# Where the slot numbers of a token sorting are computed: four instructions go from VectorE to GpSimd, and the sorting's parts are dealt out over the steps in another way

## The chip, the core and the metric

The kernel runs on one core of a Trainium2 chip. A core has TensorE (matrix products and transposes), VectorE, ScalarE and GpSimd (elementwise work and reductions), and SyncE, whose queue issues most DMAs. In the profile they are PE, DVE, ACT, POOL and SP; PEld is TensorE's loading of weights. The metric is device time of one execution in microseconds.

## The reference

A block of two layers on x of 2 x 2048 tokens of 512 features, with a context of 2 x 128 tokens. Each layer adds an attention over the context and a feed-forward part. Layer 0's feed-forward is quantised; layer 1's sends each token to one of eight experts:

```python
x = x + _L0_xattn_ref(_layernorm(x), ctx, ctx, ...)      # rope, tanh, causal, 16 heads of 64
x = x + _L0_ffn_ref(_layernorm(x), ...)                  # fake-quantised silu(gate) * up
x = x + _L1_xattn_ref(_layernorm(x), ctx, ctx, mask, ...)  # 16 heads of 32
x = x + _L1_ffn_ref(_layernorm(x), Wg, bg, We, be)

def _L1_ffn_ref(x, Wg, bg, We, be):
    probs = jax.nn.softmax(x @ Wg + bg, axis=-1)         # 512 classes
    idx = jnp.argmax(probs, axis=-1)
    p = jnp.take_along_axis(probs, idx[..., None], axis=-1)[..., 0]
    e_idx = idx % 8                                      # the expert of a token
    h = jax.nn.relu(jnp.einsum('bsd,edf->besf', x, We) + be[None, :, None, :])
    onehot = jax.nn.one_hot(e_idx, 8)
    return jnp.einsum('besf,bse->bsf', h, onehot) * p[..., None]
```

## The kernel before

The 4096 tokens are 32 tiles of 128 (`NT = 32`). Layer 0 comes first, then layer 1's attention, one tile per step of the loop `for n in range(NT)` (L1226), then the experts. The profile's steps below are this loop's n.

**A step of layer 1's loop.** `scores(n)` makes 16 heads' scores on TensorE (L892), and VectorE takes them from PSUM with the mask (L900) and finds the maxima (L905), each in two halves. `exponentials(n)` is on ScalarE (L914). `shares(n, half)` sums on VectorE (L920, first half only), takes reciprocals (L922), and multiplies on GpSimd (L923, one instruction per half). `turned(n)` transposes the result on TensorE (L116) and copies it back on ScalarE (L931), `mixed(n)` applies it to the values (L941). In between stand the work of tiles before and after: `queries` for the next block of two tiles (L872), `projected(n - 1)` (L955, L956), `biased(n - 1)`, which adds a bias on GpSimd (L949), `normed2(n - 1)` and `normed(n + 4 or n + 5)` (L92, L94, L100 and L821 on VectorE, with a power on GpSimd in L101 between them), `split` and `joined` (L826 on VectorE, a transposing DMA L829, L832 on ScalarE), `logits`, `picked` and `gated` for tile n - 2 (L978, L984 to L1008). `gated` ends in a reciprocal (L1008) and the write of the tile's row to `x_dram`; its count of tokens per expert is one GpSimd instruction (L1004). L1008 is the last of VectorE's ordinary instructions in a step.

**The sorting.** Tokens have to be gathered by expert. It is done twice: `routing(True)` (L1050) for the first 22 tiles (`NTA`), over the last steps of the loop, and `routing(False)` for all 32, during the experts. `routing` is a Python generator, and each `yield` ends one part. In `routing(True)` the parts are:

1. Ranks by three matmuls (L1056 to L1059), copied to SBUF (L1061, L1063).
2. Tiles per expert and their sums, on 8 columns (L1030 to L1073; L1030 and L1031 are a helper that divides and rounds down).
3. Which expert each gathered tile has (L1085 to L1092).
4. The slot numbers on 128 x 22 x 8 (L1096 to L1099), their sum over the experts (L1100), and its quotient and remainder (L1030, L1031, L1102) on 22 columns.
5. Two parts with one-hot rows of the quotient (L1111, L1115, L1118 each).
6. Three parts with one-hot rows of the remainder (L1124: twice 1024 columns, then 768).
7. 22 matmuls that turn these into token numbers (L1132) and four small instructions (L1134 to L1138).

The caller, at the end of a step, deals the parts out: three at step 24, two at each step after. So step 24 has parts 1 to 3; step 25 has 4 and the first of 5; step 26 the second of 5 and the first of 6; step 27 the other two of 6; step 28 has 7, and then the first four gathers (`gathered`, L1149, issued by GpSimd).

**What sets the order.** TensorE, VectorE, ScalarE and GpSimd work in manual order (`manual_schedule`): each engine's instructions stand in the order in which the Python code emits them, and each engine takes them strictly in turn. A part of the sorting that step n emits at its end is therefore ahead of everything of step n + 1 on its engine. The buffers of the sorting are columns of token tiles that have already been written to `x_dram` (`part`, L1017), so no other work shares them.

Of the kernel before, what the change touches and what calls it, by code (L numbers as in the profile page):

```python
# [19 lines left out]
ALU = mybir.AluOpType  # L20
# [4 lines left out]
P = 128  # L25
# [11 lines left out]
NE = 8  # L37
# [5 lines left out]
NTA = 22  # L43
# [6 lines left out]
NOWHERE = float(2**20)  # L50
# [13 lines left out]
def two_layers(ctx: ExitStack, tc: tile.TileContext, a, out):  # L64
    nc = tc.nc
# [85 lines left out]
    with ExitStack() as l0:  # L151
# [176 lines left out]
        def normed(k):  # L328


            stats[k] = small.tile([P, NB0, 2], F32, name="stat")
            for t, n in enumerate(tiles[k]):
                mv = variance(xs[n])
                ve = small.tile([P, 1], F32, name="ve")
                nc.vector.tensor_scalar(ve, mv[:, 1:2], 1.0 + EPS, EPS * EPS, ALU.mult, ALU.add)
                nc.vector.tensor_copy(stats[k][:, t, 0:1], mv[:, 0:1])
                nc.gpsimd.tensor_tensor(stats[k][:, t, 1:2], ve, minus_half, ALU.pow)
            if k > 1:
                features_in(k)
                turned_in(k)  # L340
# [42 lines left out]
        def queries(u, par):  # L383

            k, g = divmod(u, NG)
            j, b = blocks[k]
            if par == 0:
                if j not in tabs:
                    tables_in(j)
                ropes[u] = [mid.tile([P, B0], F32, name=f"rt{i}", bufs=1) for i in range(4)]  # L390
            pq, rt = psm.tile([P, B0], F32, name="pq", tag="m"), ropes[u]
            for c in range(ND):
                nc.tensor.matmul(  # L393
                    pq, wqs[c // 2][:, c % 2, par, g * P : (g + 1) * P], xnTs[k][:, c, :], start=(c == 0), stop=(c == ND - 1)
                )
            cos, sin = tabs[j]
            if par == 0:
                nc.vector.tensor_tensor(rt[0], pq, cos, ALU.mult)  # L398
                nc.vector.tensor_tensor(rt[1], pq, sin, ALU.mult)
                return  # L400
            qs[u] = [mid.tile([P, B0], F32, name=f"q{i}") for i in range(2)]
            nc.vector.tensor_tensor(rt[2], pq, sin, ALU.mult)  # L402
            nc.gpsimd.tensor_tensor(qs[u][0], rt[0], rt[2], ALU.subtract)  # L403
            nc.vector.tensor_tensor(rt[3], pq, cos, ALU.mult)
            nc.gpsimd.tensor_tensor(qs[u][1], rt[3], rt[1], ALU.add)

        def scores(u):

            k, g = divmod(u, NG)
            j, b = blocks[k]  # L410
            for par, k_ in ((0, kTe), (1, kTo)):
                for h in range(4):
                    rows = slice(32 * h, 32 * h + 32)
                    nc.tensor.matmul(  # L414
                        sc[:, h, :B0], k_[rows, g, b * T : (b + 1) * T], qs[u][par][rows, :],
                        start=(par == 0), stop=(par == 1), tile_position=(32 * h, 0),
                    )
            prs[u] = pr = mid.tile([P, 4, B0], F32, name="pr")
            nc.scalar.activation(pr, sc[:, :, :B0], AF.Tanh, scale=1.0 / (math.sqrt(DH0) * GROK))  # L419

            nc.scalar.activation(pr, pr, AF.Exp, bias=pad[:, b : b + 1], scale=GROK)
            if j == 0:
                nc.gpsimd.affine_select(
                    out=pr[:, :, :P], in_=pr[:, :, :P], pattern=[[0, 4], [1, P]],
                    compare_op=ALU.is_ge, fill=0.0, base=0, channel_multiplier=-1,
                )
# [60 lines left out]
        with tc.manual_schedule(engines={E.PE, E.DVE, E.Activation, E.Pool}):  # L487
# [20 lines left out]
            for u in range(nu + 2):  # L508
# [34 lines left out]
                if g in (0, NG - 1) and u > 1:  # L543
                    if makes and not loaded:
                        load_, args, _, _ = makes[0]
                        loaded.append(load_(*args))
                    elif makes:
                        _, _, make, args = makes.pop(0)
                        turns[u + 1] = make(loaded.pop(), *args)
                        if makes:  # L550
                            load_, args, _, _ = makes[0]
# [63 lines left out]
    hot = w1.tile([P, NT, NE], BF16, name="hot")  # L615
# [21 lines left out]
    with ExitStack() as up:  # L637
# [100 lines left out]
        for blk in range(NT // NBF):  # L738
            for i in range(NI):
# [20 lines left out]
                n = (blk + 1) * NBF + t  # L760
# [3 lines left out]
                if i >= 3 and i % 2 == 1:  # L764
                    n = (blk + 1) * NBF + (i - 3) // 2
# [182 lines left out]
    def biased(n):  # L948
        nc.gpsimd.tensor_tensor(xs[n], xs[n], bob, ALU.add)  # L949
# [67 lines left out]
    def part(n, shape, dtype=F32, at=0):  # L1017

        size = math.prod(shape)
        v = xw[n][:, at : at + (size * mybir.dt.size(dtype) + 3) // 4]  # L1020
        if dtype is not F32:
            v = v.bitcast(dtype)[:, :size]
        if len(shape) == 1:
            return v
        names = "abc"[: len(shape)]
        return v.rearrange(f"p ({' '.join(names)}) -> p {' '.join(names)}", **dict(zip(names, shape)))
# [6 lines left out]
    def along(k):  # L1033

        return part(16, [NE], at=NE * k)
# [14 lines left out]
    def routing(first):  # L1050

        nt, nj = (NTA, NJA) if first else (NT, NJB)
# [7 lines left out]
        rank = part(15, [nt, NE])  # L1060
        nc.vector.tensor_copy(rank, prank)  # L1061
        cnt, tl, base = along(1), along(2), along(3)
        nc.vector.tensor_copy(cnt, pc)  # L1063
        yield
        if first:
# [8 lines left out]
            base = start  # L1074
# [18 lines left out]
        yield  # L1093
        slot, pos, sj, ss = part(20, [nt, NE]), part(16, [nt], at=128), part(16, [nt], at=192), part(16, [nt], at=256)
        limb = lim.unsqueeze(1).to_broadcast([P, nt, NE])
        nc.vector.tensor_tensor(slot, rank, limb, ALU.is_ge if first else ALU.is_lt)  # L1096
        nc.vector.scalar_tensor_tensor(slot, slot, NOWHERE, rank, ALU.mult, ALU.add)
        nc.vector.tensor_tensor(slot, slot, base.unsqueeze(1).to_broadcast([P, nt, NE]), ALU.add)
        nc.vector.tensor_tensor(slot, slot, hot[:, :nt, :], ALU.mult)  # L1099
        nc.vector.tensor_reduce(pos, slot, AX.X, ALU.add)  # L1100
        floor_div(sj, pos, P)
        nc.vector.scalar_tensor_tensor(ss, sj, -float(P), pos, ALU.mult, ALU.add)  # L1102
# [123 lines left out]
    for n in range(NT):  # L1226
        blk, t = n // NB1, n % NB1
        ahead = blk + 1 < nblk
        fs = range(t * ND // NB1, (t + 1) * ND // NB1)
        if n > 0:  # L1230
            biased(n - 1)
        firsts = [m for m in (n + 2 * NB1, n + 2 * NB1 + 1) if m < NT and (m >= TURNED) == (m > n + 2 * NB1)]
        firsts = [normed(m) for m in firsts]
        scores(n)
        if 4 <= n < 4 + 2 * NE and n % 2 == 0:

            nc.scalar.dma_start(out=rowadd, in_=v_dram[(n - 4) // 2].partition_broadcast(P))

        late = t == 0 and n > 1
        if ahead and not late:  # L1240
            queries(blk + 1, fs[:1])
        if late:
            logits(n - 2)
        exponentials(n)
        if ahead and late:
            queries(blk + 1, fs[:1])
        if n == 0:
            for i in range(NT - held, NT - held + 2):
                down(i)
                widened(i + 2)  # L1250
        shares(n, 0)
        if n > 1:
            if not late:
                logits(n - 2)
            picked(n - 2)
        shares(n, 1)
        if n > 0:
            projected(n - 1)
            normed2(n - 1)()
        firsts = [first() for first in firsts]  # L1260
        rest = gated(n - 2) if n > 1 else None
        if n + 1 < NT:
            kept_keys(n + 1)
        for first in firsts:
            if first:
                first()
        if 0 < n <= NE:
            load(we[:, n - 1], a["L1_ffn_We"][n - 1].rearrange("(c p) f -> p c f", p=P))
        if ahead:
            queries(blk + 1, fs[1:])  # L1270
        if n == 0:
            for i in range(NT - held + 2, NT):
                down(i)
            dwn.close()
            ffd.close()
            moe = ctx.enter_context(tc.tile_pool(name="moe", bufs=1, side="right"))
            we = moe.tile([P, NE, ND, D], F32, name="we")
        if 4 <= n < 4 + 2 * NE:
            e, half = divmod(n - 4, 2)
            for c in range(2 * half, 2 * half + 2):  # L1280
                nc.gpsimd.tensor_tensor(we[:, e, c, :], we[:, e, c, :], rowadd, ALU.add)
        if not ahead:

            expert(n - NT + NB1)
        turned(n)
        if rest:
            rest()
        if n > 0:
            turned2(n - 1)
        mixed(n)  # L1290
        if t == NB1 - 1 and blk + 2 < nblk:
            for t in range(NB1):
                turned1((blk + 2) * NB1 + t)
        if n == NTA + 2:
            route = routing(True)
        if route:
            for _ in range(3 if n == NTA + 2 else 2):
                if next(route, route) is route:
                    route = None
                    for j in range(4):  # L1300
                        gathered(j)
                    break
        if n == NT - NB1 - 1:
            for j in range(3):
                centered_x(j)
            turned_x2(0)
# [59 lines left out]
```

## Time and profile before

| | |
|---|---|
| median of 3 runs | 1602.42 us (1600.16 to 1602.53) |
| the profiled execution | 1603.67 us, its span 1601.9 us |
| busy in the span | TensorE 97%, VectorE 74%, ScalarE 45%, GpSimd 36% |
| layer 0 and its feed-forward, up to the first score matmul of layer 1's loop | 0 to 930.44 us |
| steps 0 to 23 of that loop | 930.44 to 1302.31 us |
| steps 24 to 27 | 1302.31 to 1371.06 us |
| steps 28 to 31 | 1371.06 to 1434.75 us |
| last logits and experts | 1434.75 to 1601.9 us |

All times inside the trace are counted from the start of the span. TensorE's busy share says little on its own, since a matmul that waits in the pipeline counts too. What one step of the loop costs is read from the distance between the first L892 of a step and of the next, and what a late engine costs from the idle time ahead of an instruction and what ended it. A group's mean can hide two lengths of the same instruction, so the single instructions of the timeline are shown where that matters.

### The profile page before, as it was taken

How to read it: one execution, taken by the hardware profiler on the slowest of the kernel's cores; microseconds unless marked ns; L12 is line 12 of the kernel's file. 1: busy time of each engine (PE TensorE's matmuls, PEld its weight loads, DVE VectorE, ACT ScalarE, POOL GpSimd, SP SyncE). 2: the span in 40 equal slices, each digit the busy share in tenths (PEclk: the TensorE clock that was granted, in tenths of full speed). 3: DMA queues.
4: the chain of work that ended last, by engine and by line, in shares of the span. 5: the costliest groups of instructions: out<-in, count | busy, mean ns of one | idle time of the engine just before them, and what ended most of it. 6: DMA issues, size and time to landing. Idle time of an engine off the chain costs nothing. (4 is left out here: it accounts for less than half of the span.)

```text
span 1601.9 us, 26167 instructions
## 1 busy us (share of the span) xinstructions
PE 1553.0 (97%) x9542; PEld 908.7 (57%) x9542; DVE 1192.1 (74%) x2336; ACT 719.7 (45%) x1537; POOL 583.7 (36%) x576
## 2 busy tenths in 40 slices
PE   7999999999999999999999999999999998999997
PEld 5655555555555555544444466666666665654443
DVE  3467777777777885689986678888888889867442
ACT  1222222222222222243335566777777766753342
POOL 2232222222222222110005653556555443544553
PEclk9999999999999999999999999999999999999999
DMA  9511212111111220467668735112211121114563
GB/s 326 182 37 41 47 40 47 40 47 42 54 41 40 67 52 1 125 176 196 182 171 279 261 140 144 34 47 38 50 47 34 40 36 32 41 47 133 159 161 88
DMA packets 180571, 150.90 MB, mean 94 GB/s; under 512 B 97089, under 2 KB 144665, under 8 KB 180444
## 3 DMA queue, kind: packets, MB, share of 16 engines
q1 hardware_dynamic: 170188, 127.25, 28.7%
q0 software_dynamic: 6240, 18.70, 3.9%
q10 hardware_dynamic: 4016, 3.29, 0.9%
q8 instruction: 76, 1.25, 0.3%
q14 instruction: 51, 0.42, 0.1%
HBM read 89.97 MB, written 41.79 MB: 82 GB/s over the span
## 5 line engine op out<-in xcount | busy, mean ns | idle before, releaser
L419 ACT ACTIVATE pr<-sc 128x1024 f32<-128x1024 f32 x64 | 65.6, 1024 | 421.6 <-PE sc L414 421.4
L393 PE MATMUL pq<-xnT,wq 128*128 128x256 f32 x1024 | 254.4, 391 | 0.0
L451 PE MATMUL pw<-wo,att 128*128 128x512 f32 x512 | 230.8, 593 | 0.0
L393 PEld LDWEIGHTS pq<-xnT,wq 128*128 128x128 f32 x1024 | 184.4, 189 | 67.1 <-issue 44.4
L914 ACT ACTIVATE s<-s,mx 128x128 f32<-128x128 f32 x512 | 175.3, 388 | 31.1 <-DVE mx L905 31.0
L923 POOL TENSOR_TENSOR s<-s,rs 128x1024 f32<-128x1024 f32 x64 | 120.9, 1903 | 151.5 <-DVE rs L922 151.1
L403 POOL TENSOR_TENSOR q<-rt,rt 128x256 f32<-128x256 f32 x64 | 46.8, 731 | 339.7 <-DVE rt L402 335.2
L451 PEld LDWEIGHTS pw<-wo,att 128*128 128x128 f32 x512 | 96.9, 190 | 96.4 <-issue 89.9
L441 DVE RECIPROCAL rd<-sc 128x256 f32<-128x256 f32 x64 | 112.4, 1757 | 46.6 <-PE sc L435 46.4
L1185 PE MATMUL pz<-we,x 128*128 x312 | 140.3, 602 | 2.3 <-ACT x L832 2.0
L872 PE MATMUL pq<-xT,wq 128*128 128x256 f32 x512 | 122.6, 382 | 0.0
L978 PE MATMUL pl<-wgate,xnT 128*128 128x512 f32 x256 | 116.7, 599 | 0.0
L955 PE MATMUL pw<-wo,oT 128*128 128x512 f32 x256 | 115.2, 592 | 0.7 <-ACT oT L946 0.7
L872 PEld LDWEIGHTS pq<-xT,wq 128*128 128x128 f32 x512 | 96.0, 190 | 33.1 <-issue 20.3
L398 DVE TENSOR_TENSOR rt<-pq,rope_cos 128x256 f32<-128x256 f32 x64 | 27.0, 422 | 104.2 <-PE pq L393 104.2
L749 ACT ACTIVATE gate<-pg,gsc 128x512 f32<-128x512 f32 x88 | 60.5, 687 | 93.2 <-PE pg L744 81.8
L1185 PEld LDWEIGHTS pz<-we,x 128*128 128x128 f32 x312 | 58.2, 192 | 70.3 <-issue 66.0
L92 DVE BATCH_NORM_STATS2 st<-x 128x6 f32<-128x512 f32 x130 | 89.3, 687 | 6.0 <-DMA x<-in_ctx 3.8
L744 PE MATMUL pu<-xqT,wuT 128*128 128x512 bf16 x352 | 90.3, 379 | 2.1 <-DVE h L752 2.0
L744 PE MATMUL pg<-xqT,wgT 128*128 128x512 bf16 x352 | 90.3, 379 | 0.0
L900 DVE SCALAR_TENSOR_TENSOR s<-sc,keep 128x1024 f32<-128x1024 f32 x64 | 78.0, 1219 | 13.4 <-PE sc L892 7.7
L810 PE MATMUL py<-wdT,hb 128*128 128x512 bf16 x352 | 78.9, 384 | 2.3 <-DVE hb L804 1.5
(221 smaller groups left out, 2777.9 us busy)
## 6 DMA issues: line engine op xcount, KB each, us to landing
h_dram<-h SPq DMA_DIRECT2D x88, 256.0 KB
hq<-h_dram SPq DMA_DIRECT2D x31, 704.0 KB
x_dram<-x SPq DMA_DIRECT2D x32, 258.0 KB
x<-in_x SPq DMA_DIRECT2D x32, 256.0 KB
we<-in_L_ffn_We SPq DMA_DIRECT2D x8, 1024.0 KB
xnT<-in_x_turned SPq DMA_DIRECT2D x14, 512.0 KB
along<-stat_dram SPq DMA_DIRECT2D x14, 256.0 KB
w_in<-in_L_ffn_w_gate SPq DMA_DIRECT2D x11, 256.0 KB
```

Of the source, the lines that this page charges most:

```text
L92: nc.vector.bn_stats(out=st, in_=x)
L393: nc.tensor.matmul(pq, wqs[c // 2][:, c % 2, par, g * P : (g + 1) * P], xnTs[k][:, c, :], start=(c == 0), stop=(c == ND - 1))
L441: nc.vector.reciprocal(rd, sc[:, 0, B0:])
L451: nc.tensor.matmul(pw, atts[u][:, f, t * P : (t + 1) * P], wo[:, 2 * g + f, :], start=(g == 0 and f == 0), stop=(g == NG - 1 and f == 1),)
L744: nc.tensor.matmul(dst, w[:, c, i * P : (i + 1) * P], xqTs[blk][:, c, :], start=(c == 0), stop=(c == ND - 1),)
L810: nc.tensor.matmul(py, hbs[n][:, i, :], wdT[:, i, :], start=(i == 0), stop=(i == NI - 1))
L872: nc.tensor.matmul(pq, wq1[:, c, f * P : (f + 1) * P], xTs[blk][:, c, :], start=(c == 0), stop=(c == ND - 1))
L914: nc.scalar.activation(s[:, h, :], s[:, h, :], AF.Exp, bias=mx[:, h : h + 1], **accum)
L923: nc.gpsimd.tensor_tensor(s, s, rs.unsqueeze(2).to_broadcast([P, 8, T]), ALU.mult)
L955: nc.tensor.matmul(pw, os_[n][:, c, :], wo1[:, c, :], start=(c == 0), stop=(c == ND - 1))
L978: nc.tensor.matmul(pl, xn2T[n][:, c, :], wgate[:, c, :], start=(c == 0), stop=(c == ND - 1))
L1185: nc.tensor.matmul(pz, ring[j][:, c, :], we[:, bass.ds(e, 1), c, :], start=(c == 0), stop=(c == ND - 1))
```

## The change

In the first sorting (`first` is true) part 4 is cut in two. The comparison stays on VectorE. The product with `NOWHERE`, the sum with the ranks, the sum with the bases and the product with the one-hot expert rows are made by GpSimd, where the first two were one VectorE instruction before. A `yield` follows, and the sum over the experts with quotient and remainder is a part by itself. There are eleven parts instead of ten. The second sorting keeps its instructions.

```diff
-        nc.vector.tensor_tensor(slot, rank, limb, ALU.is_ge if first else ALU.is_lt)
-        nc.vector.scalar_tensor_tensor(slot, slot, NOWHERE, rank, ALU.mult, ALU.add)
-        nc.vector.tensor_tensor(slot, slot, base.unsqueeze(1).to_broadcast([P, nt, NE]), ALU.add)
-        nc.vector.tensor_tensor(slot, slot, hot[:, :nt, :], ALU.mult)
+        baseb = base.unsqueeze(1).to_broadcast([P, nt, NE])
+        if first:
+            nc.vector.tensor_tensor(slot, rank, limb, ALU.is_ge)
+            nc.gpsimd.tensor_scalar(slot, slot, NOWHERE, None, ALU.mult)
+            nc.gpsimd.tensor_tensor(slot, slot, rank, ALU.add)
+            nc.gpsimd.tensor_tensor(slot, slot, baseb, ALU.add)
+            nc.gpsimd.tensor_tensor(slot, slot, hot[:, :nt, :], ALU.mult)
+            yield
+        else:
...
         nc.vector.tensor_reduce(pos, slot, AX.X, ALU.add)
...
-            for _ in range(3 if n == NTA + 2 else 2):
+            for _ in range({NTA + 2: 4, NTA + 3: 1}.get(n, 2)):
```

With four parts at step 24 and one at step 25 the parts fall so:

| end of step | before | after |
|---|---|---|
| 24 | 1, 2, 3 | 1, 2, 3, comparison and GpSimd's four |
| 25 | 4, first of 5 | sum, quotient, remainder |
| 26 | second of 5, first of 6 | both of 5 |
| 27 | second and third of 6 | first and second of 6 |
| 28 | 7, gathers | third of 6, 7, gathers |

On GpSimd the four instructions stand behind L1004 of step 24 and ahead of L949 of step 25. On SyncE's queue nothing changes its place.

More of the change, by code (lines that the diff above doesn't have):

```diff
@@ L1095, in routing @@
         limb = lim.unsqueeze(1).to_broadcast([P, nt, NE])
-        nc.vector.tensor_tensor(slot, rank, limb, ALU.is_ge if first else ALU.is_lt)
-        nc.vector.scalar_tensor_tensor(slot, slot, NOWHERE, rank, ALU.mult, ALU.add)
-        nc.vector.tensor_tensor(slot, slot, base.unsqueeze(1).to_broadcast([P, nt, NE]), ALU.add)
-        nc.vector.tensor_tensor(slot, slot, hot[:, :nt, :], ALU.mult)
+        baseb = base.unsqueeze(1).to_broadcast([P, nt, NE])
[7 more added lines that the diff above has]
+        else:
+            nc.vector.tensor_tensor(slot, rank, limb, ALU.is_lt)
+            nc.vector.scalar_tensor_tensor(slot, slot, NOWHERE, rank, ALU.mult, ALU.add)
+            nc.vector.tensor_tensor(slot, slot, baseb, ALU.add)
+            nc.vector.tensor_tensor(slot, slot, hot[:, :nt, :], ALU.mult)
         nc.vector.tensor_reduce(pos, slot, AX.X, ALU.add)
```

## The prediction

> **What bounds the kernel now.** The page first: TensorE is busy for 97% of the span, so elsewhere only work on TensorE counts. The change lies in the last steps of layer 1's loop, so the next view is the busy time of each engine in stretches, cut where each step's score matmuls (L892) start. The columns are stretch, length, busy time (and instructions) of PE, PEld, DVE, ACT and POOL, granted clock, DMA share, GB/s. The six lines are steps n = 23 to 28.
>
> ```profile
> span 1601.9 us, 26167 instructions
> PE 1553.0 (97%) x9542; PEld 908.7 (57%) x9542; DVE 1192.1 (74%) x2336; ACT 719.7 (45%) x1537; POOL 583.7 (36%) x576
> ```
>
> ```profile
> 1286.99:1302.31 15.32, 15.24 (x117) 10.15 (x116) 13.19 (x30) 10.42 (x34) 6.69 (x8) 1.00 0.26 36
> 1302.31:1317.89 15.58, 15.50 (x120) 10.35 (x119) 13.24 (x29) 12.90 (x37) 6.97 (x8) 1.00 0.25 35
> 1317.89:1335.71 17.82, 15.45 (x119) 9.93 (x117) 15.71 (x44) 10.34 (x34) 6.23 (x6) 1.00 0.20 31
> 1335.71:1355.56 19.85, 16.90 (x120) 11.24 (x116) 17.88 (x43) 12.87 (x36) 7.90 (x8) 0.91 0.11 28
> 1355.56:1371.06 15.50, 15.21 (x120) 10.01 (x116) 13.91 (x27) 10.61 (x34) 5.93 (x5) 1.00 0.15 37
> 1371.06:1387.03 15.97, 15.89 (x142) 10.77 (x139) 12.01 (x25) 13.30 (x37) 6.67 (x6) 1.00 0.09 33
> ```
>
> An undisturbed step takes 15.32 us and TensorE fills it. Steps 25, 26 and 27 take 17.82, 19.85 and 15.50: together 7.21 us more than three plain ones, and in 25 and 26 VectorE's busy time is longer than a plain step. Who holds TensorE there, from its timeline (start, duration, instruction, idle before it and what ended it):
>
> ```profile
> 1330.88 1.09 PE L116 MATMUL pt<-ident,s 128*128 128x128 f32 x8 [1.30 <-POOL s L923]
> 1332.76 1.09 PE L116 MATMUL pt<-ident,s 128*128 128x128 f32 x8 [0.78 <-POOL s L923]
> 1349.73 1.23 PE L116 MATMUL pt<-ident,s 128*128 128x128 f32 x8 [2.33 <-POOL s L923]
> 1351.58 1.97 PE L116 MATMUL pt<-ident,s 128*128 128x128 f32 x8 [0.62 <-POOL s L923]
> ```
>
> The transposes wait for L923 on GpSimd, and that had itself waited 5.98 and 5.97 us for VectorE's reciprocals (L922). So VectorE is late, because the routing's parts stand in its queue at the end of steps 24 to 26, ahead of the next step's score eviction (L900). The slowest of them, on VectorE and on GpSimd:
>
> ```profile
> 1318.44 0.49 DVE L1030 TENSOR_SCALAR x<-x 128x8 f32<-128x8 f32 x1
> 1335.90 0.33 DVE L1096 TENSOR_TENSOR x<-x,x 128x176 f32<-128x176 f32 x1
> 1336.26 1.31 DVE L1097 SCALAR_TENSOR_TENSOR x<-x,x 128x176 f32<-128x176 f32 x1
> 1337.60 0.34 DVE L1098 TENSOR_TENSOR x<-x,x 128x176 f32<-128x176 f32 x1
> 1338.72 0.18 DVE L1030 TENSOR_SCALAR x<-x 128x22 f32<-128x22 f32 x1
> 1340.07 0.68 DVE L92 BATCH_NORM_STATS2 st<-x 128x6 f32<-128x512 f32 x1
> 1356.49 1.21 DVE L1124 TENSOR_TENSOR x<-t,x 128x1024 bf16<-128x1024 bf16 x1
> ```
>
> ```profile
> 1317.63 1.27 POOL L949 TENSOR_TENSOR x<-x,bob 128x512 f32<-128x512 f32 x1
> 1322.40 0.55 POOL L101 TENSOR_TENSOR r<-ve,minus_half 128x1 f32<-128x1 f32 x1 [3.50 <-DVE ve L100]
> 1335.94 1.43 POOL L949 TENSOR_TENSOR x<-x,bob 128x512 f32<-128x512 f32 x1
> ```
>
> L1097 takes 1.31 us here and 0.42 on 256 columns in the second sorting: it starts inside GpSimd's L949 and ends 0.2 us after it. L1030 takes 0.49 inside the other L949 and 0.18 when GpSimd is idle. Some VectorE forms are held while GpSimd computes; L900 (1.22) and the reductions L905 (1.22) are the same beside a GpSimd instruction or not.
>
> **How lateness turns into time.** In a plain step L900 starts 1.32 us after the step's first score matmul; here after 4.36, 5.37, 2.06 and 1.30 in steps 25 to 28, late by D = 3.04, 4.05, 0.74 and 0. The second half of the transposes starts 12.40 after that first matmul in a plain step and 14.86 in step 25, so 0.58 of D is free: loss = D - 0.58 + 0.04, which gives 2.50 and 0.20 for steps 25 and 27 (measured 2.50 and 0.18). From L900 to the end of VectorE's ordinary work (start of L1008) pass 13.58 us in steps 25 and 26, 12.31 in step 27. In the late steps VectorE has hardly a gap: its work sets the pace, and what it saves comes off the end until it has caught up (in step 28 it waits 0.29 us for TensorE).
>
> **The change part by part**, for VectorE's tail behind L1008.
> - End of step 24. The comparison moves here: 0.36 (L1096's start to L1097's). Its four GpSimd products and sums stand ahead of L949 in GpSimd's queue, and wait for it, so L949 is no longer running beside L1030 at 1318.44, which gets back 0.30 (0.52 to the next start, against 0.22 at 1338.72). Net +0.06: D25 = 3.10, loss 2.56.
> - GpSimd's four instructions on 128x176. The trace has no such shape; L403 on 128x256 takes 0.73, L949 on 128x512 1.27, so 2.1 ns a column and 0.56 for 176. I take that, as the nearest row by size; ends 0.20 (the shortest 128x8 one, L1004) and 1.90 (L923, 128x1024 with a broadcast). They start some 3.45 us into step 25 and end at 5.7. Behind them L949 (1.27) and L101 (0.55) end at 7.5, and L923 is wanted at 11.08, when VectorE's reciprocal is there: hidden by 3.6 us. L949's result is wanted by L956 at 1330.55, also later. In that time VectorE runs L92, L94, the one-column L100, L900 and L905, which the trace shows unheld beside GpSimd. Cost nothing; without that cover 4 x 0.56 = 2.2 us.
> - End of step 25. Of VectorE's 4.24 us from L1008 to L92 (1335.83 to 1340.07) the comparison, L1097 to L1099 and the three instructions of the first one-hot go. What stays: the sum L1100, 0.37, then L1030. Held by L949, as the 128x8 one was, it ends 0.03 behind L949's end (1.38 after L1008), then 0.34 more: 1.75. Saved 2.49. If its 22 columns are not held, the tail is 0.97 and 3.27 is saved. I take held, by the row of the same line. L900 then starts 0.12 + 1.75 + 1.01 = 2.88 into step 26: D26 = 1.56, loss 1.02 against 4.53.
> - End of step 26. Both one-hots (the first held by L949 as before, the second 0.36 + 0.25 + 0.21) instead of one and the 1.13 of L1124: 0.31 saved. But step 26 ends earlier too, so VectorE stands 0.12 behind its end, where it was 0.90 ahead. L900 starts 0.12 + 2.65 = 2.77 into step 27: D27 = 1.45, loss 0.91 against 0.18. Part of the gain is given back here.
> - End of step 27. Two full L1124 (2.34) instead of one full and one of 768 (2.07): 0.27 more, inside the 0.29 that VectorE waits. L949 behind it on GpSimd starts that much later; L956 wants it 9 us on.
> - Step 28. The short L1124 (0.95) now stands ahead of the 22 matmuls of L1132. VectorE was idle there for 1.98 us waiting for them. It ends some 1.0 us after L1008 (1385.00), at 1386.0 by the old times; L1132 starts at 1386.38, and only its last six want it, 0.5 us on. Nothing, and if it is held by GpSimd's L1004 (0.20 to 0.65) still nothing. The gathers keep their place behind it in GpSimd's queue, the DMAs of SP's queue their order: planes and x rows only move with their step.
> Sum: losses 2.56 + 1.02 + 0.91 = 4.49 against 7.21, a gain of 2.72 us. VectorE's own sum agrees: 0.06 - 2.49 - 0.31 = -2.74. The profiled execution took 1603.67 us (span 1601.9), 1.25 above the median of 1602.42; so 1600.95 for such a one, and 1599.7 on the runs.
>
> **Two rules of the skill.** Step 26 ran at a granted clock of 0.91, that is 3.41 us at half clock, from 1351.42 on: the second batch of transposes took 1.97 us instead of 1.09. In my sum that costs nothing beyond what VectorE loses anyway, for without it step 26 would be 18.83 and step 27 16.46, 35.3 in both cases. The Trainium skill ("TensorE: Matmul & The Clock Gate", part 1) has the clock halved by an idle activity window of 3.4 us and the loss at half of the throttled time; by it 1.7 us come on top, and the sum would be 4.4. The Trainium skill ("GPSIMD Engine Reference", 4.1) says of elementwise work with two inputs that GpSimd takes about twice VectorE's time and that VectorE is to be used: 0.34 against 0.56 us in my rows agrees, and by it the move would cost 4 x 0.22 = 0.9 us if both stood on one path; here L923's 5.98 us of waiting hides it.
>
> **The rivals.**
> - L1030 is not held in step 25 (22 columns, no row of that width beside GpSimd): D26 = 0.78, losses 2.56 + 0.24 + 0.91 = 3.71, gain 3.5, 1598.9. For: the one-column L100 and L986 are unheld. Against: L1030 at 128x8.
> - The half clock was paid for in full. TensorE's idle time in step 26 falls from 2.95 to about 1.1 us, too little for a drop, and half of 3.41 us comes on top: gain 4.4, 1598.0. Against: VectorE has no gap in steps 26 and 27 that TensorE's speed could close.
> - What VectorE saves is taken up again by step 27 and by the second sorting: gain near 0, 1602.4. For: 0.73 us do come back in step 27. Against: L900 starts on time in step 28.
> - GpSimd becomes late (slower). If one of its four instructions takes X, L949 and L101 behind them let L923 start when 4X > 5.8 us, so X above 1.45; the gain is gone at X = 2.1, and at X = 2.9 the loss is 3.2 us: 1605.6. For: no row has their shape. Against: L923's 128x1024 takes 1.90.
>
> **How the numbers follow.** 0.2% is 3.2 us, about what a measurement of this kernel can tell from no change; the three runs lie 2.4 us apart. Forecast 0.60, L1030 free 0.15, half clock 0.07, no gain 0.12, GpSimd late 0.06. The forecast's 2.7 us lies 0.5 short of the bound, with runs that scatter by about 1 us: a third of its chance counts as faster (0.20), with 0.09 of the second and 0.06 of the third: 0.35. Slower is the last, 0.05; the rest, 0.60, is within. The range goes from the half-clock case, 1597.8, to nearly no gain, 1601.9; the likeliest case alone has 1598.7 to 1600.7.
>
> **What would show it.** Steps 25, 26 and 27 of 17.9, 16.3 and 16.2 us; no half clock in step 26; L1097 gone from the first sorting, four GpSimd instructions of about 0.56 us near 1321.5; L1030 in step 25 of about 1 us, held by L949; step 28 at 15.97. Wrong if L923 in step 25 starts on GpSimd's account, if L1030 takes 0.18, or if TensorE waits at L1132 for L1124.

## The result, and the profile after

The changed kernel takes 1599.05 us (median of 21 runs, 1596.23 to 1601.79), the kernel before 1601.24 us beside it (21 runs, 1597.66 to 1603.43). The ratio is 0.9987, with a 95% interval from 0.9981 to 0.9993: 2.2 us faster by the medians, 1.1 to 3.0 by the interval. That is less than 0.2%, and more than nothing.

The profiled execution took 1599.43 us, its span 1597.4. In the changed kernel the comparison is L1099, GpSimd's four are L1100 to L1103, the sum is L1110, the one-hots are L1121, L1125 and L1128, then L1134, and the 22 matmuls are L1142. Its steps 24 to 28 in the view of stretches, with the columns as before (length, busy time of the five rows, granted clock, DMA share, GB/s):

```profile
1302.38:1317.96 15.58, 15.50 (x121) 10.34 (x120) 13.26 (x29) 12.91 (x37) 6.75 (x7) 1.00 0.23 35
1317.96:1336.89 18.93, 16.92 (x119) 11.05 (x117) 16.81 (x48) 10.43 (x34) 9.96 (x11) 0.91 0.12 29
1336.89:1352.20 15.31, 15.14 (x120) 10.15 (x116) 13.68 (x31) 12.82 (x36) 5.66 (x6) 1.00 0.14 36
1352.20:1368.40 16.20, 15.23 (x117) 10.00 (x116) 14.51 (x32) 10.61 (x34) 6.82 (x6) 1.00 0.14 36
1368.40:1384.37 15.97, 15.89 (x143) 10.78 (x139) 13.14 (x26) 13.29 (x37) 7.71 (x6) 1.00 0.09 32
```

Steps 25 to 27 take 50.45 us against 53.17, that is 2.72 less. Single steps are not the ones forecast: the half-clock stretch that lay in step 26 now lies in step 25 (granted clock 0.91), which takes 18.93, and step 26 takes 15.31.

The spans differ by more, 4.5 us (1601.9 and 1597.4). Up to step 25 the new one is 0.06 later, steps 25 to 27 save 2.72, steps 28 to 31 take 63.69 in both, and behind them 167.15 us became 165.31. That last 1.84 can't be put down to the change. Counted from the start of step 31 to the end of the span, that stretch took between 180.5 and 183.3 us in the ten traces of this study, in no order that follows the edits, and 1.84 lies within that scatter. Whoever reads the gain off two spans gets 4.5, which happens to be the rival with the half clock paid in full; the steps and the medians both contradict it.

On TensorE, the transposes and what they wait for (start, duration, instruction, idle before it):

```profile
1330.89 1.09 PE L116 MATMUL pt<-ident,s 128*128 128x128 f32 x8 [1.25 <-POOL s L923]
1332.75 1.51 PE L116 MATMUL pt<-ident,s 128*128 128x128 f32 x8 [0.76 <-POOL s L923]
1334.13 1.08 PE L116 MATMUL pt<-ident,xn 128*128 128x128 f32 x4
...
1365.45 1.09 PE L116 MATMUL pt<-ident,s 128*128 128x128 f32 x8 [0.68 <-POOL s L923]
```

The wait in step 25 is what it was (1.25 and 0.76, before 1.30 and 0.78), the one of 2.33 and 0.62 in step 26 has gone, and 0.68 in step 27 is new. From 1333.28 on, by the record of the granted clock, the transposes run at half clock: 1.51 us for eight instead of 1.09, 1.08 for four instead of 0.63.

VectorE and GpSimd, from their timelines:

```profile
1318.50 0.17 DVE L1030 TENSOR_SCALAR x<-x 128x8 f32<-128x8 f32 x1
1335.90 0.32 DVE L1110 TENSOR_REDUCE x<-x 128x22 f32<-128x176 f32 x1
1336.25 0.98 DVE L1030 TENSOR_SCALAR x<-x 128x22 f32<-128x22 f32 x1
1337.58 0.68 DVE L92 BATCH_NORM_STATS2 st<-x 128x6 f32<-128x512 f32 x1
```

```profile
1321.40 0.67 POOL L1100 TENSOR_SCALAR x<-x 128x176 f32<-128x176 f32 x1 [3.68 <-DVE x L1099]
1322.16 0.56 POOL L1101 TENSOR_TENSOR x<-x,x 128x176 f32<-128x176 f32 x1
1322.79 0.56 POOL L1102 TENSOR_TENSOR x<-x,x 128x176 f32<-128x176 f32 x1
1323.43 0.52 POOL L1103 TENSOR_TENSOR x<-x,hot 128x176 f32<-128x176 f32 x1
1323.91 1.27 POOL L949 TENSOR_TENSOR x<-x,bob 128x512 f32<-128x512 f32 x1
1328.94 3.75 POOL L923 TENSOR_TENSOR s<-s,rs 128x1024 f32<-128x1024 f32 x2 [3.24 <-DVE rs L922]
1335.93 1.27 POOL L949 TENSOR_TENSOR x<-x,bob 128x512 f32<-128x512 f32 x1
```

The L949 that ran at the turn from step 24 to 25 has moved behind GpSimd's four, and L1030 beside its old place takes 0.17 instead of 0.49. At the end of step 25 L1030 on 22 columns starts inside L949 and ends 0.03 us after it: 0.98 instead of 0.18. GpSimd is done with all of it 3.24 us before L923 is wanted.

The Trainium skill ("SBUF — State Buffer", section "SBUF: two separate sides") has VectorE and GpSimd share one pair of ports under an exclusive lock, taken by a VectorE instruction that reads two SBUF tensors or runs in a two-port mode. The rows agree. L905, with one input, takes its 1.22 us beside L1103 and L949 at 1323.52. L1110, also with one, starts 0.03 us before L949 and leaves that at 1.27, where L1096 with two inputs, in the same place before, went with an L949 of 1.43. L1097 has two inputs and was held. L1030 has one input and is held, so by that page it would be in a two-port mode, which no row here shows. It also holds in the other direction: in step 28 GpSimd's L1004 takes 0.98 us beside L1134, where it took 0.20 before, at no cost.

### The profile page after: what moved, and what is told of

Read it like the earlier page. It is cut to its first block, busy times and chain, and to the rows that moved or that the text cites. A ratio compares the mean times of both kernels' runs of the same rounds, so it can differ in the third digit from the quotient of the medians.

```text
span 1597.4 us, 26167 instructions
## 1 busy us (share of the span) xinstructions
PE 1551.3 (97%) x9542; PEld 909.1 (57%) x9542; DVE 1192.5 (75%) x2333; ACT 720.4 (45%) x1537; POOL 586.8 (37%) x580
## 3 DMA queue, kind: packets, MB, share of 16 engines
q8 instruction: 76, 1.25, 0.3%
## 5 line engine op out<-in xcount | busy, mean ns | idle before, releaser
L923 POOL TENSOR_TENSOR s<-s,rs 128x1024 f32<-128x1024 f32 x64 | 120.9, 1903 | 149.6 <-DVE rs L922 149.1
L92 DVE BATCH_NORM_STATS2 st<-x 128x6 f32<-128x512 f32 x130 | 89.4, 688 | 6.0 <-DMA x<-in_ctx 3.8
L900 DVE SCALAR_TENSOR_TENSOR s<-sc,keep 128x1024 f32<-128x1024 f32 x64 | 78.1, 1220 | 14.3 <-PE sc L892 9.1
L955 PEld LDWEIGHTS pw<-wo,oT 128*128 128x128 f32 x256 | 48.6, 190 | 55.3 <-issue 53.6
```

The lines of the kernel that those rows point to most:

```text
L92: nc.vector.bn_stats(out=st, in_=x)
L900: nc.vector.scalar_tensor_tensor(s, sc[:, 2 * half : 2 * half + 2].rearrange("p r c k -> p (r c) k"), -MASKED, keeps[n].unsqueeze(1).to_br ...
L923: nc.gpsimd.tensor_tensor(s, s, rs.unsqueeze(2).to_broadcast([P, 8, T]), ALU.mult)
L955: nc.tensor.matmul(pw, os_[n][:, c, :], wo1[:, c, :], start=(c == 0), stop=(c == ND - 1))
```

## Experiments

Each run changes one of the two kernels of the case. Steps 25 to 27 are compared by their sum in the trace (before 53.17, changed kernel 50.45), because single executions of one kernel scatter by 5 us and more. Each trace is one execution. The first four runs and the last four were on two different chips, each with runs of the kernel before on the same chip. The ratios are estimated from all these runs, so they are not the quotient of the two medians and differ from it by up to 0.0007.

### The dealing alone

```diff
         if first:
             nc.vector.tensor_tensor(slot, rank, limb, ALU.is_ge)
-            nc.gpsimd.tensor_scalar(slot, slot, NOWHERE, None, ALU.mult)
-            nc.gpsimd.tensor_tensor(slot, slot, rank, ALU.add)
-            nc.gpsimd.tensor_tensor(slot, slot, baseb, ALU.add)
-            nc.gpsimd.tensor_tensor(slot, slot, hot[:, :nt, :], ALU.mult)
+            nc.vector.scalar_tensor_tensor(slot, slot, NOWHERE, rank, ALU.mult, ALU.add)
+            nc.vector.tensor_tensor(slot, slot, baseb, ALU.add)
+            nc.vector.tensor_tensor(slot, slot, hot[:, :nt, :], ALU.mult)
             yield
```

> The sorting's parts cut and dealt out as in the changed kernel, but the three instructions stay on VectorE. Theory (VectorE's queue sets the pace in steps 25 to 27, so its tails count one for one): the tail of step 24 grows by 1.1 us of arithmetic and by the 0.3 us for which L949 again holds L1030; steps 25, 26 and 27 take 19.3, 16.3 and 16.2 us, 51.8 together, which is 1.3 below before (53.17) and 1.4 above the change (50.45). Rival 1 (the dealing alone makes the gain): 50.4 to 50.5, as the change. Rival 2 (the gain is the clock drop that left step 26): any total between 52 and 53.2, by where a drop falls. Where a half-clock window falls in a step, the theory has the sum of the three unchanged.

The three steps in the view of stretches:

```profile
1316.53:1336.82 20.29, 16.85 (x118) 11.33 (x116) 18.05 (x51) 10.43 (x34) 7.32 (x7) 0.92 0.17 27
1336.82:1352.14 15.32, 15.08 (x120) 10.10 (x116) 13.62 (x30) 12.83 (x36) 5.67 (x6) 1.00 0.14 36
1352.14:1368.41 16.27, 15.23 (x118) 9.96 (x117) 14.58 (x32) 10.60 (x34) 6.89 (x6) 1.00 0.14 36
```

Together 51.87 by the unrounded starts, as forecast (51.8), although a half-clock stretch in step 25 deals them out in another way. L1100, the former L1097, takes 0.34 here, since L949 has ended by then. So, by the steps, 1.3 of the 2.72 us come from dealing, 1.4 from GpSimd. The median is 1600.28 against 1602.35, ratio 0.9992 (0.9982 to 1.0001), which alone would decide nothing.

### GpSimd alone

```diff
             nc.gpsimd.tensor_tensor(slot, slot, hot[:, :nt, :], ALU.mult)
-            yield
...
-            for _ in range({NTA + 2: 4, NTA + 3: 1}.get(n, 2)):
+            for _ in range(3 if n == NTA + 2 else 2):
```

> The four instructions on GpSimd, but in one part with the sum behind them, dealt out as before. Theory: VectorE waits for GpSimd's 2.55 us inside step 25's tail, and L949 behind them holds L1030; L92 starts 5.5 us after L1008 instead of 4.24. Steps 25, 26, 27: 17.8, 20.1, 16.5, together 54.4, 1.3 us slower than before. Rival 1 (the dealing makes all of the gain): 53.2, as before. Rival 2 (taking work off VectorE is enough, wherever it is awaited): some 52 to 52.5.

The steps, and VectorE's wait in step 25's tail:

```profile
1320.32:1338.12 17.80, 15.44 (x118) 9.92 (x117) 15.69 (x44) 10.33 (x34) 6.20 (x6) 1.00 0.20 31
1338.12:1359.93 21.81, 17.91 (x120) 12.32 (x117) 17.05 (x40) 13.00 (x36) 10.50 (x12) 0.84 0.10 25
1359.93:1375.25 15.32, 15.23 (x121) 10.16 (x117) 13.85 (x28) 10.44 (x34) 5.75 (x6) 1.00 0.16 43
```

```profile
1341.30 0.34 DVE L1109 TENSOR_REDUCE x<-x 128x22 f32<-128x176 f32 x1 [2.67 <-POOL x L1103]
```

Together 54.93 us, 1.8 slower than before, and by the runs 1603.32 against 1602.35, ratio 1.0010 (1.0001 to 1.0019). The forecast was 54.4; 0.3 of the difference is a wait of 0.29 us ahead of L900 that the trace gives no releaser for. By the steps, the dealing alone gains, GpSimd alone loses, and together they gain more than the dealing: here GpSimd's work is worth something only where a step's work of VectorE lies between it and the instruction that reads it. A step is what the added yield buys.

### L949 moved, in the kernel before

```diff
-        if n > 0:
+        if 0 < n < NTA + 3 or n > NTA + 6:
             biased(n - 1)
         firsts = [m for m in (n + 2 * NB1, n + 2 * NB1 + 1) if m < NT and (m >= TURNED) == (m > n + 2 * NB1)]
         firsts = [normed(m) for m in firsts]
+        for m in {NTA + 3: [n - 1], NTA + 4: [n - 1, n, n + 1]}.get(n, []):
+            biased(m)
```

> The kernel before, with GpSimd's bias instruction L949 of steps 25 to 28 moved behind the next step's first L101, into the stretch of L900 and L905 (those of tiles 25 to 27 together at step 26). Nothing is left out. Theory (L949 holds L1030, L1097 and L1115 for 0.30, 0.97 and 0.95 us): these three take 0.17, 0.34 and 0.33 us; steps 25, 26, 27 take 17.5, 17.9, 15.6, together 51.0, 2.2 below before. Rival (the long L1097 and L1115 have another cause, such as their own shape, and L949 only happens to run beside them): they stay at 1.3 us and the sum at 53.2.

The instructions that were 1.31 and 1.28 us long are L1097 of step 25's end, shown ahead of the result, and L1115 of step 26's end, in the kernel before:

```profile
1355.08 1.28 DVE L1115 TENSOR_TENSOR x<-x,t 128x165 bf16<-128x165 bf16 x1
```

The steps, and the same two instructions with L949 moved:

```profile
1317.97:1335.48 17.51, 15.45 (x119) 9.93 (x117) 15.41 (x44) 10.33 (x34) 6.46 (x6) 1.00 0.21 31
1335.48:1353.34 17.86, 15.58 (x121) 9.91 (x117) 15.92 (x40) 12.78 (x36) 9.17 (x9) 1.00 0.12 31
1353.34:1368.92 15.58, 15.23 (x120) 10.01 (x117) 13.95 (x30) 10.62 (x34) 5.59 (x5) 1.00 0.14 37
```

```profile
1336.03 0.34 DVE L1097 SCALAR_TENSOR_TENSOR x<-x,x 128x176 f32<-128x176 f32 x1
...
1353.88 0.33 DVE L1115 TENSOR_TENSOR x<-x,t 128x165 bf16<-128x165 bf16 x1
```

Together 50.95 us (forecast 51.0): the hold by L949 was all of the extra length, and moving one GpSimd instruction in four steps is worth 2.2 us in steps 25 to 27, nearly as much as the change of this case. The median is 1599.47 against 1602.35, ratio 0.9989 (0.9980 to 0.9998).

### L949 moved, in the changed kernel

The same edit; this is the run after_bias.

> The changed kernel with the same move of L949. Nothing is left out. Theory: L1030 of step 25 falls from 0.98 to 0.18 and the first L1125 from 1.28 to 0.33; steps 25, 26, 27 take 17.9, 15.6, 15.4, together 48.8, 1.65 below the change and 4.4 below before: some 1596.9 us. Rival (TensorE's waits or the clock pace these steps, not VectorE's tail): 50.4, as the change. Rival 2 (three L949 in a row in step 26 delay L923): step 26 above 16.

```profile
1318.62:1337.53 18.91, 16.91 (x119) 11.09 (x117) 16.71 (x51) 10.44 (x34) 9.05 (x10) 0.91 0.12 29
1337.53:1352.84 15.31, 15.23 (x120) 10.15 (x116) 13.14 (x29) 12.75 (x36) 9.19 (x8) 1.00 0.14 36
1352.84:1368.16 15.32, 15.17 (x118) 10.16 (x117) 13.66 (x32) 10.50 (x34) 5.52 (x5) 1.00 0.16 41
```

```profile
1336.91 0.18 DVE L1030 TENSOR_SCALAR x<-x 128x22 f32<-128x22 f32 x1
1338.85 1.22 DVE L900 SCALAR_TENSOR_TENSOR s<-sc,keep 128x1024 f32<-128x1024 f32 x1 [0.33 <-PE sc L892]
```

L1030 and L1125 fall to 0.18 and 0.33. But the sum is 49.54, not 48.8. Step 25 has a half-clock stretch again, and steps 26 and 27 are plain ones with no room to make up for it: in step 26 VectorE waits at L900 for TensorE's scores. The median is 1596.94 against 1602.35, ratio 0.9968 (0.9958 to 0.9979): faster than before, and its interval lies outside that of the changed kernel.

### TensorE kept busy in its wait

The half clock was the suspect for the missing 0.75 us, so this run fills TensorE's wait in step 25 of the last kernel with matmuls made twice.

```diff
-    def queries(blk, fs):
+    def queries(blk, fs, again=1):
...
-            for c in range(ND):
+            for c in [*range(ND)] * again:
                 nc.tensor.matmul(
                     pq, wq1[:, c, f * P : (f + 1) * P], xTs[blk][:, c, :], start=(c == 0), stop=(c == ND - 1)
                 )
...
-            queries(blk + 1, fs[1:])
+            queries(blk + 1, fs[1:], 2 if n == NTA + 3 else 1)
```

> The kernel of the run after_bias with the second half of step 25's query matmuls made twice (same inputs, same result, 1.73 us), so that TensorE computes where it waited for L923. In the look at after_bias steps 25 to 27 took 49.54, 0.75 above my 48.8, and a half-clock window lay over the end of step 25. Theory (the drop follows the idle time, and costs where VectorE catches up): no half clock in steps 25 and 26, step 25 still about 17.9, the three 48.8. Rival (the 0.75 is from the three L949 in step 26, or the clock costs nothing here): 49.5, or 50.5 if the added matmuls count on the path.

```profile
1317.25:1335.01 17.76, 16.96 (x127) 11.54 (x125) 15.66 (x45) 10.46 (x34) 8.80 (x10) 1.00 0.12 31
1335.01:1350.56 15.55, 15.22 (x120) 10.01 (x117) 13.79 (x33) 12.94 (x36) 9.17 (x9) 1.00 0.27 35
1350.56:1365.95 15.39, 15.10 (x120) 10.00 (x116) 13.68 (x32) 10.52 (x34) 5.58 (x5) 1.00 0.15 37
```

```profile
1332.05 1.09 PE L116 MATMUL pt<-ident,s 128*128 128x128 f32 x8 [0.51 <-POOL s L923]
```

TensorE's waits for L923 in step 25, 1.24 and 0.76 us in after_bias, are none and 0.51 here. No half clock, and 48.70 us: 0.84 less than without the added work. The rivals, three L949 in a row or a price for the added matmuls, fall. The median is 1599.29 against 1603.69, ratio 0.9976 (0.9967 to 0.9985), not better than the kernel without the filling (0.9968, on the other chip): the two traces show what a stretch costs when it falls here, and by the last section it need not fall here in every execution.

### How far GpSimd's cover reaches

Four and twelve more sums behind GpSimd's four, into columns that nothing reads:

```diff
             nc.gpsimd.tensor_tensor(slot, slot, hot[:, :nt, :], ALU.mult)
+            spare = part(19, [nt, NE])
+            for _ in range(4):
+                nc.gpsimd.tensor_tensor(spare, rank, baseb, ALU.add)
             yield
```

> The changed kernel with four more sums on 128x176 behind GpSimd's four (into columns that nothing reads). The changed kernel's rows have 2.55 us for the four and leave GpSimd 3.24 us idle ahead of L923 in step 25. Theory (that idle time is the cover, to the last tenth): four more take 2.5 us, L923 still starts when VectorE's reciprocal is there, steps 25 to 27 stay at 50.4 to 50.5 and GpSimd's idle ahead of L923 falls to 0.7. Rival (GpSimd's work costs on the path, by the port that it holds or by L949 and L101 that it puts off): 1 to 2.5 us more in steps 25 to 27.

> The same with twelve more, 7.6 us, that is 4.3 us beyond the idle time. Theory: L923 of step 25 starts 4.3 us later, VectorE waits behind it at L821, and steps 25 to 27 take 54.8 us; the kernel is 1.6 us slower than before. Rival (GpSimd's lateness is absorbed further on): 50.4 to 52.

With four more, the steps and what is left of GpSimd's idle time ahead of L923:

```profile
1317.88:1335.62 17.74, 15.44 (x118) 9.93 (x116) 15.65 (x45) 10.34 (x34) 10.96 (x14) 1.00 0.20 31
1335.62:1351.99 16.37, 15.46 (x120) 9.91 (x116) 14.61 (x33) 12.78 (x36) 6.73 (x7) 1.00 0.13 34
1351.99:1368.33 16.34, 15.27 (x120) 9.92 (x116) 14.65 (x32) 10.61 (x34) 6.95 (x6) 1.00 0.14 35
```

```profile
1328.87 3.75 POOL L923 TENSOR_TENSOR s<-s,rs 128x1024 f32<-128x1024 f32 x2 [0.81 <-DVE rs L922]
```

With twelve more, and VectorE's waits in step 25:

```profile
1319.79:1343.34 23.55, 18.06 (x119) 12.38 (x117) 17.29 (x48) 10.54 (x34) 16.88 (x23) 0.86 0.15 24
```

```profile
1334.56 0.69 DVE L956 TENSOR_TENSOR x<-x,pw 128x512 f32<-128x512 f32 x1 [2.08 <-POOL x L949]
1339.31 0.75 DVE L821 SCALAR_TENSOR_TENSOR xn<-x,mv 128x512 f32<-128x512 f32 x1 [2.87 <-POOL x L101]
```

Twice GpSimd's work costs nothing: 50.46 us by the unrounded starts, the changed kernel's sum. Its ratio is 0.9987 (0.9978 to 0.9996). Four times the work passes the cover by 4.3 us, and the sum is 54.97 (forecast 54.8), ratio 1.0017 (1.0007 to 1.0027). Ahead of L821 VectorE first waits at L956 for the delayed L949, a wait that the forecast had not named. The run with four more has no half clock in these steps, and shows the changed kernel's steps as they are without one: 17.74, 16.37, 16.34. The sum is the same as with one.

### The sorting begun a step earlier

On top of the moved L949:

```diff
-        if n == NTA + 2:
+        if n == NTA + 1:
             route = routing(True)
...
-            for _ in range({NTA + 2: 4, NTA + 3: 1}.get(n, 2)):
+            for _ in range({NTA + 3: 1}.get(n, 2)):
```

> The changed kernel with L949 moved as in the run after_bias, and the first sorting begun a step earlier (parts 1 and 2 at step 23, part 3, the comparison and GpSimd's four at step 24, then one, two, two and the last two as before). Nothing is left out. Theory (VectorE's tails add up until it has caught up, and a step more gives it about 0.7 us of spare time): losses of 1.4, 0.4, 0.2 and 0.1 us in steps 24 to 27; steps 23 to 27 take 79.0 us, against 81.3 for the change, 80.4 for after_bias in its look and 84.1 for before: some 1.5 us less than after_bias, 5 to 6 less than before. Rival (what is left in after_bias is not VectorE's queue): 80.4 or more.

Steps 23 to 27:

```profile
1286.11:1301.69 15.58, 15.50 (x120) 10.35 (x120) 13.25 (x29) 10.59 (x35) 6.94 (x8) 1.00 0.24 35
1301.69:1318.82 17.13, 15.59 (x119) 9.91 (x117) 15.10 (x41) 12.61 (x36) 6.23 (x6) 1.00 0.21 32
1318.82:1334.42 15.60, 15.23 (x121) 10.01 (x117) 13.89 (x33) 10.61 (x34) 9.05 (x11) 1.00 0.26 35
1334.42:1349.96 15.54, 15.21 (x120) 10.00 (x116) 13.78 (x33) 12.94 (x36) 9.17 (x9) 1.00 0.14 35
1349.96:1365.36 15.40, 15.11 (x121) 10.02 (x117) 13.70 (x32) 10.52 (x34) 5.60 (x5) 1.00 0.15 38
```

Together 79.25 us (forecast 79.0), against 84.07 before, 81.34 for the change and 80.44 for after_bias in its trace. Most of the 1.19 us less than after_bias is the half-clock stretch, which this trace doesn't have: the run with TensorE kept busy, also without one, takes 79.59 in the same steps. So the step more is worth some 0.3 us, and the 1.5 of the forecast compared with a trace that had the stretch in it. The median is 1598.74 against 1603.69, ratio 0.9969 (0.9958 to 0.9980). In the steps it is the shortest of all; by the runs it can't be told from after_bias (0.9968, on the other chip). Both beat the two kernels of the case.

## Why the prediction was right

- **What bounds.** VectorE's queue sets the pace in steps 25 to 27, and its tails count one for one: seven edits (the change, the dealing alone, L949 moved in the kernel before, four and twelve more sums, the earlier sorting, and TensorE kept busy) moved the sum of these steps, or of 23 to 27, by -4.8 to +1.8 us and came within 0.25 us of what their tails add up to. Two runs missed, GpSimd alone by 0.5 and after_bias by 0.75, and in both a half-clock stretch fell where VectorE had caught up with TensorE. For after_bias the run with TensorE kept busy shows that the stretch is the cause. For GpSimd alone 0.29 of the miss is the wait without a releaser, and that the rest is the stretch over the end of step 26 is not shown.
- **The sum.** 2.72 us were forecast for steps 25 to 27 and 2.72 measured. The median moved by 2.2, its interval holds 2.72. The time was forecast as 1599.7 and is 1599.05. Since the forecast was made against the first three runs (1602.42) and the 21 have a median of 1601.24, part of that agreement is luck: the gain is what was forecast well, not the level.
- **End of step 24.** The comparison (0.33) and L1030 freed (0.17): L92 starts at 1321.23 in both traces, that is 0.06 earlier, net of the shift, where 0.06 later was forecast: the comparison, priced at 0.36, pushed L92 back by 0.25 only.
- **GpSimd's four.** The three with two inputs took 0.56, 0.56 and 0.52 as forecast, the product with a constant 0.67, and from the first start to L949 it is 2.51 us instead of 2.2. The cover was 3.24 instead of 3.6. Nothing of it reached TensorE, and another 2.5 us didn't either.
- **End of step 25.** The choice between a held and a free L1030 was the widest open end. It was held (0.98), and L92 started 1.75 us after L1008, as forecast. The free case's 3.5 us would have needed the move of L949.
- **Ends of steps 26 and 27, step 28.** L900 starts 2.75 us into step 27 (forecast 2.77), 1.30 into step 28, which takes 15.97. TensorE doesn't wait at L1142.
- **The half clock.** Wrong by place, right by price. Forecast were 17.9, 16.3 and 16.2 us; measured 18.93, 15.31 and 16.20, because the stretch fell in step 25, whose waits the change leaves alone. The prediction looked for a stretch in step 26 only. That it costs nothing beside VectorE's lateness was right for this kernel (34.24 us for steps 25 and 26 with it, 34.11 without), and is no general truth: in after_bias it cost 0.84. The Trainium skill ("TensorE: Matmul & The Clock Gate", part 1) takes half of the throttled time as the loss, 1.7 us for 3.41; measured were 0.1 and 0.84, and 1.56 in an earlier step (last section), so its figure is an upper end here.
- **The rivals.** The gain was not taken up again by the second sorting as far as the scatter behind step 31 lets one see. The late GpSimd is real, but begins only beyond some 5.8 us of added work (2.51 and the 3.24 of cover), where the change has 2.5.

## What to carry to other kernels

What these runs bear out for one kernel: when one engine's queue sets the pace for a few steps, add up its tails, the idle time another engine spends waiting for it, and the slack that is left before it counts; the sum over the steps holds even where single steps are shuffled by the clock, as long as that engine is behind. Work moved to a slower engine was free with a whole step between it and its reader, and worse than before with the reader right behind it. And look for an instruction of the sharing engine beside every VectorE instruction that is longer than its own size explains: moving that one was worth nearly as much here as moving the work.

## What was not expected of the hardware

The half-clock stretches last 3.41 us, or twice that where TensorE had waited longest (3.90 us in step 26 with GpSimd alone, 5.49 us in step 25 with twelve more sums), and fall in other places from one trace to the next. In the ten traces one lay near 911 us in four, near 962 us in three, and none in either place in four (one trace has both); the same 2.0 us of gaps in step 25 led to a stretch in the changed kernel and to none with four more sums on GpSimd.

The traces fit one rule. Within each of them the stretches start whole multiples of 3.413 us apart: in the changed kernel those at 961.23, 1333.28 and 1480.05 us by 109 and by 43 of them. Cut each trace into windows on this grid of its own, from 40 us to the end of the loop, and add up what TensorE's matmuls leave idle in each. All 13 windows with 1.79 us or more are followed by a stretch; of those with 1.76 or less only two are, each of them the first half of one of the long stretches. By this a window need not be wholly idle, and the place of the grid decides: in step 25 of the changed kernel a window ends at 1333.28 with 1.79 us idle, with four more sums one ends at 1333.47 with 1.53. Behind the loop two windows don't fit (1.64 us with a stretch, 1.89 without).

In steps 0 to 22, 1.56 us are lost where a stretch falls near 962 us: from the start of step 0 to that of step 23 it is 358.1 us with it and 356.6 without. That alone makes executions differ by more than half of what this change gains.

On GpSimd a product with a constant, one input and 176 columns, took longer (0.67 us) than a sum of two inputs of that size (0.56).
